# A two-layer graph network on one core: first destinations by way of SBUF, and ten groups of q and v rows instead of five

## The chip, the core and the metric

The kernel runs on one core of one Trainium2 chip. A core has TensorE (PE, with its weight loads listed apart as PEld), VectorE (DVE), ScalarE (ACT), GpSimd (POOL) and SyncE (SP), each with an instruction queue of its own, and 16 DMA engines that all queues share. SBUF and PSUM are its on-chip memories of 128 partitions; tables lie in HBM. The metric is the device time of one execution in microseconds. Other measurements of the text come from one profiled execution.

## What is computed

There are 30,000 nodes with 128 features and 960,000 edges, sorted by destination. Cut to what matters:

```python
# layer 0: two relational convolutions, 32 edge types made of 8 bases
h   = relu(layernorm(x))
W   = einsum('rb,bdf->rdf', coeff, basis)
agg = segment_sum((h @ W[etype32])[src] * norm, dst)     # once, relu, once more
x   = x + agg2
# layer 1: gated convolution, 4 edge types
h   = relu(layernorm(x))
k, q, v = h @ Wk[t] + bk[t], h @ Wq[t] + bq[t], h @ Wv[t] + bv[t]
msg = sigmoid(k[dst] + q[src]) * v[src]                  # of the edges with edge_type_4 == t
agg_t = segment_sum(msg, dst)
x   = x + mean over t of (agg_t + h @ Ws[t] + b[t])
```

Everything is float32. (The masked sum over t lets each edge take only the tables of its own type.)

## The kernel before

Edges are cut into tiles of 128 and groups of three tiles (384 edges). Since edges are sorted, the destinations of a group lie in a window of 32 nodes that begins at the group's first destination; a short preparation checks this, and a slower path, not taken here, stands ready in the other case. Sums are held in one SBUF tile `agg` [128 features x nodes] and a group's result is added at columns `agg[:, base : base + 32]` (`add_windows`, line 356). `base` is known only at run time, so it has to be in a register of the engine that uses it.

Three passes over all edges follow each other (`edge_pass`, lines 727 to 729): c1 and c2 are the two relational convolutions (`rel_body`), g is the gated one (`gate_body`). A pass is a loop of 25 iterations of 100 groups. An iteration is cut into four stages of 25 groups, a stage into five blocks of five groups (index `s`; `S = SB = 5`). The order of the instructions on every engine is written out by hand (`manual_schedule`), and the loop has the staggered kind of iteration sync: engines may be in neighbouring stages, `stage_boundary` marks where one begins and `leave_stage` where each engine waits until it is done with the one before.

At the beginning of a stage `loads(k + 1)` asks on SP's queue for the next stage's tiles of indices and relative destinations (`stage_tile`, one tile of each name per stage, `bufs=NQ=4`). `bases` (line 345) brings the first destinations of a stage's 25 groups from row `i*NQ + k` of `first_st` in HBM to 25 registers of one engine:

- in c1 and c2 on DVE, at the fourth group of a stage's second block (group 8 of 25);
- in g on DVE, at the fifth group of a stage's first block (group 4), and once more on SP in `window` (line 478), which fetches a group's 128 key rows (`kw`) from the k table, five groups ahead.

In c1 and c2 a group is: POOL gathers three times 128 rows of h by index (`hg`, line 114, 5 buffers of a group each); DVE builds for each tile a selection matrix times coefficients (`sb`, line 439, 12 buffers); PE multiplies (`pa`); ACT copies to `ab`; once per block PE multiplies by the bases (`po`, line 407) and two blocks later DVE adds the windows.

In g a group is: POOL gathers three times 128 rows of q and v (`qv[n]`, 1 KB a row, 5 buffers of a group each, line 533); PE selects keys by a one-hot matrix (`keys`, line 499, from `kb` that DVE makes of a broadcast 960 KB load per block, `onehot`, line 486); DVE adds q (line 540); ACT takes the sigmoid (line 541). Two groups later DVE multiplies by v (`msg`, line 508), which is the last use of `qv[n]`, and PE sums (`po`, line 510). So DVE's order in iteration step n is: add of group n, product of group n - 2, then, by position in the block, one-hot, windows, `bases`.

Beside the groups run the steps of the node work of the pass before (`beside`), 120 nodes at a time.

Of the kernel before, what the change touches and what calls it, by code (L numbers as in the profile page):

```python
# [9 lines left out]
F32 = mybir.dt.float32  # L10
# [21 lines left out]
G = 3  # L32
# [37 lines left out]
def kernel(  # L70
# [223 lines left out]
    def sorted_path():  # L294
        with ExitStack() as all_:
# [46 lines left out]
                nc.sync.dma_start(t, array[:, ds(i * (NQ * NTS) + k * NTS, NTS + more)])  # L342
                return t

            def bases(i, k, engine):
                _, vals = nc.values_load_multi_w_load_instructions(
                    first_st[ds(i * NQ + k, 1), :NGS], engines=[engine],
                    min_val=0, max_val=N - 1, skip_runtime_bounds_check_because=IN_RANGE)
                return vals

# [10 lines left out]
            def rel_body(table, weights, cof):  # L361
                def start(npool):
                    bas = npool.tile([P, B, D], F32, name="bas")
                    nc.scalar.dma_start(bas, weights.rearrange("b d f -> d b f"))
                    return lambda *args: body(bas, *args)

                def body(bas, i, io, pool, ps, cp, iw, ic, beside):
                    stage = {}
                    er, oh, pc, ce, ab, po, base = {}, {}, {}, {}, {}, {}, {}

                    def loads(k):
                        stage[k] = [stage_tile(io, "idx", src, I32, i, k),
                                    stage_tile(io, "relc", reld, F32, i, k),
                                    stage_tile(io, "nrm", norm, F32, i, k, 4 * TQ - S * G)]

                    def types(s):
                        er[s] = pool.tile([P, TQ, TP], I32, name="er")
                        nc.sync.dma_start(
                            er[s].rearrange("p c e -> p (c e)"),
                            bass.AP(tensor=et32_row.tensor, offset=(i * NG + s * S) * GE,  # L380
                                    ap=[[TQ * TP, 4], [0, R], [1, TQ * TP]]))

                    def onehot(s):
                        oh[s] = pool.tile([P, TQ, TP], F32, name="oh")
                        nc.vector.tensor_scalar(oh[s], er[s], icol4, None, op0=ALU.is_equal)
                        at = (1 + s % 2) * TQ * 4 * B
                        pc[s] = cp[:TP, at:at + TQ * 4 * B].rearrange("p (c q b) -> p c q b",
                                                                      c=TQ, q=4)
                        for c in range(TQ):
                            nc.tensor.matmul(pc[s][:, c].rearrange("p q b -> p (q b)"),  # L390
                                             lhsT=oh[s][:, c, :],
                                             rhs=cof.rearrange("p q b -> p (q b)"),
                                             start=True, stop=True)

                    def coefficients(s):
                        ce[s] = pool.tile([TP, 4, TQ, B], F32, name="ce")
                        t0 = s % SB * S * G
                        nrm = stage[s // SB][2][:, t0:t0 + 4 * TQ]
                        nc.vector.tensor_mul(
                            ce[s], pc[s].rearrange("p c q b -> p q c b"),  # L400
                            nrm.rearrange("p (q c) -> p q c", q=4).unsqueeze(3).to_broadcast(
                                [TP, 4, TQ, B]))

                    def bases_out(s):
                        po[s] = ps.tile([P, S, W], F32, name="po")
                        for b in range(B):
                            nc.tensor.matmul(po[s].rearrange("p s w -> p (s w)"),  # L407
                                             lhsT=bas[:, b, :],
                                             rhs=ab[s][:, b].rearrange("p s w -> p (s w)"),
                                             start=(b == 0), stop=(b == B - 1))  # L410

                    loads(0)
                    types(0)
                    onehot(0)
                    coefficients(0)
                    types(1)
                    onehot(1)
                    for s in range(NS):
                        k = s // SB
                        if s % SB == 0:  # L420
                            if s:
                                tc.stage_boundary()
                            if k + 1 < NQ:
                                loads(k + 1)
                        if s % SB == 2:
                            leave_stage()
                        idx, relc, _ = stage[k]
                        if s + 2 < NS:
                            types(s + 2)
                        ab[s] = pool.tile([P, B, S, W], F32, name="ab")  # L430
                        for g in range(S):
                            t0 = (s % SB * S + g) * G
                            hg = pool.tile([TP, G, D], F32, name="hg", bufs=5)
                            for j in range(G):
                                gather(hg[:, j, :], table, idx[:, t0 + j:t0 + j + 1])
                            pa = ps.tile([P, B, W], F32, name="pa", bufs=3)
                            for j in range(G):
                                sb = pool.tile([TP, B, W], F32, name="sb", bufs=12)
                                nc.vector.scalar_tensor_tensor(  # L439
                                    sb, iw[:TP].unsqueeze(1).to_broadcast([TP, B, W]),  # L440
                                    relc[:, t0 + j:t0 + j + 1],
                                    ce[s].rearrange("p q c b -> p (q c) b")[
                                        :, g * G + j, :].unsqueeze(2).to_broadcast([TP, B, W]),
                                    op0=ALU.is_equal, op1=ALU.mult)
                                nc.tensor.matmul(pa.rearrange("p b w -> p (b w)"),  # L445
                                                 lhsT=hg[:, j, :],
                                                 rhs=sb.rearrange("p b w -> p (b w)"),
                                                 start=(j == 0), stop=(j == G - 1))
                            nc.scalar.copy(ab[s][:, :, g, :], pa)  # L449
                            if g == 1 and s:  # L450
                                bases_out(s - 1)
                            if g == 2 and s + 1 < NS:
                                coefficients(s + 1)
                            if g == 3 and s + 2 < NS:
                                onehot(s + 2)
                            if g == 3 and s > 1:
                                add_windows(po[s - 2], base[(s - 2) // SB], s - 2)
                            if g == 3 and s % SB == 1:
                                base[k] = bases(i, k, DVE)
                            beside(s * S + g)  # L460
                    bases_out(NS - 1)
                    for s in (NS - 2, NS - 1):
                        add_windows(po[s], base[NQ - 1], s)
                return start

            def gate_body(i, io, pool, ps, cp, iw, ic, beside):
# [1 line left out]
                kb, kw, sel, pk, qv, po, base, kbase = {}, {}, {}, {}, {}, {}, {}, {}  # L468

                def loads(k):  # L470
                    stage[k] = [stage_tile(io, *a, i, k) for a in (
                        ("qi", qidx, I32), ("relc", reld, F32))]

                def types(s):
# [3 lines left out]
                def window(n):  # L478
                    k = n // NGS
                    if n % NGS == 0:  # L480
                        kbase[k] = bases(i, k, SP)
                    kw[n] = pool.tile([P, D], F32, name="kw", bufs=10)
                    nc.sync.dma_start(kw[n], ktab[ds(kbase[k][n % NGS] * T, P), :])

                def onehot(s):
# [2 lines left out]
                                            ALU.is_equal)  # L488
                    sel[s] = pool.tile([TP, S * G, W], F32, name="sel", bufs=3)
                    t0 = s % SB * S * G  # L490
                    relc = stage[s // SB][1][:, t0:t0 + S * G]
                    nc.vector.tensor_tensor(
                        sel[s], iw[:TP].unsqueeze(1).to_broadcast([TP, S * G, W]),
                        relc.unsqueeze(2).to_broadcast([TP, S * G, W]), ALU.is_equal)
# [25 lines left out]
                for n in range(NG):  # L520
# [9 lines left out]
                        types(s + 1)  # L530
                    if n + S < NG:
                        window(n + S)
                    qv[n] = pool.tile([TP, G, 2, D], F32, name="qv", bufs=5)
                    t0 = n % NGS * G
                    for j in range(G):
                        gather(qv[n][:, j].rearrange("p a f -> p (a f)"), qvtab,
                               stage[k][0][:, t0 + j:t0 + j + 1])
                    if n + 1 < NG:
                        keys(n + 1)
                    nc.vector.tensor_add(pk[n], pk[n], qv[n][:, :, 0, :])  # L540
# [5 lines left out]
                    if g == 4 and s:  # L546
                        add_windows(po[s - 1], base[(s - 1) // SB], s - 1)
                    if g == 4 and s % SB == 0:
                        base[k] = bases(i, k, DVE)
                    beside(n)  # L550
                sums(NG - 2)
                sums(NG - 1)
# [409 lines left out]
```

## Time and profile before

| | |
|---|---|
| Time, median of 3 runs | 28,902.54 us (28,895.52 to 28,908.87) |
| The profiled execution's own time | 34,449.25 us |
| Its span, first to last instruction | 34,447.5 us |
| Mean granted clock of TensorE | 0.674 (0.74 in c1, 0.78 in c2, 0.51 in g) |
| Gathers of POOL in c1, c2, g | 192.6 to 11,387.4; 11,431.9 to 22,748.0; 22,865.2 to 34,419.9 us |
| POOL busy in the three stretches | 7149, 7118, 7109 us |
| DMA engines' mean busy share | 0.23, 0.26, 0.47 |
| PE busy in g | 6756 of 11,555 us |

A line of the page's groups names source line, engine, operation, what is written and read, the count, then busy time and the mean of one in ns, then the idle time just before and what ended most of it. In the waits, a row is who waited for whom, the total in us, how often, and the longest. A timeline's line has start, duration, engine, line, operation, and in brackets the idle time before it and its releaser. "issue" means that the profile shows nothing that was waited for, "remote" that the releasing semaphore is known but not the instruction. A busy gather on POOL is the time in which POOL works on it, not the time until the rows have landed.

### The profile page before, as it was taken

To read this page: it belongs to the slowest core of one execution; us is meant where nothing else is said; L and a number is where in the kernel's file an instruction comes from. 1 tells how busy PE (TensorE), PEld (TensorE's weight loads), DVE (VectorE), ACT (ScalarE), POOL (GpSimd) and SP (SyncE) were. 2 spreads that over 40 slices of the span, in tenths; PEclk is the share of its full clock that TensorE was granted. 3 is DMA by queue.
4 is the path that set the end of the run, shared out by engine and by line. 5 is a ranking of instruction groups with operands and counts; after the bars stand their busy time and mean duration, and the time that the engine had idled before them with its cause. 6 is when DMAs were issued, how large, how long until landed. Compare 5 with 4: busy or idle time off the path is not lost. (4 is left out here: it accounts for less than half of the span.)

```text
span 34447.5 us, 320361 instructions
## 1 busy us (share of the span) xinstructions
PE 20497.2 (60%) x87408; PEld 17662.1 (51%) x87408; DVE 12592.8 (37%) x33274; ACT 3659.3 (11%) x9905; POOL 21410.1 (62%) x22514
## 2 busy tenths in 40 slices
PE   4555555555555566666666666665555555555555
PEld 3444544444444445545555454445555555555555
DVE  3333333333333333333333333333333333333333
ACT  1000000000000111111111111111111111111111
POOL 5666666666666566666666666656666666666666
PEclk7777777777777777777777777765555555555555
DMA  3222222222222222222222222234444444444444
GB/s 97 62 62 62 63 61 62 63 63 62 62 62 62 70 73 73 73 74 72 72 73 73 73 73 73 73 107 145 145 144 144 144 144 146 145 144 144 146 143 141
DMA packets 2182999, 3244.35 MB, mean 94 GB/s; under 512 B 551918, under 2 KB 1559594, under 8 KB 2181290
## 3 DMA queue, kind: packets, MB, share of 16 engines
q0 software_dynamic: 840000, 1967.52, 20.6%
q1 hardware_dynamic: 993620, 1001.65, 9.0%
q10 hardware_dynamic: 347670, 254.20, 2.6%
q8 instruction: 852, 13.96, 0.2%
q14 instruction: 857, 7.02, 0.1%
HBM read 2969.29 MB, written 252.28 MB: 94 GB/s over the span
## 5 line engine op out<-in xcount | busy, mean ns | idle before, releaser
L114 POOL DMA_INDIRECT hg<-h,idx x15000 | 14273.0, 952 | 8446.5 <-issue 4105.1
L445 PE MATMUL pa<-sb,hg 128*128 128x256 f32 x30000 | 9304.2, 468 | 5934.2 <-issue 2892.9
L445 PEld LDWEIGHTS pa<-sb,hg 128*128 128x128 f32 x30000 | 6919.2, 240 | 7715.2 <-issue 3346.1
L114 POOL DMA_INDIRECT qv<-qvtab,qi x7500 | 7109.3, 948 | 4562.6 <-issue 2220.3
L439 DVE SCALAR_TENSOR_TENSOR sb<-cp,relc,ce 128x256 f32<-128x256 f32 x15000 | 6134.1, 476 | 6576.0 <-remote 4679.9
L510 PE MATMUL po<-sel,msg 128*128 128x32 f32 x15000 | 3471.0, 388 | 4592.1 <-DVE msg L508 3824.5
L510 PEld LDWEIGHTS po<-sel,msg 128*128 128x128 f32 x15000 | 3420.4, 328 | 4894.5 <-DVE msg L508 3986.6
L499 PE MATMUL pk<-kw,kb 128*128 128x128 f32 x15000 | 3973.5, 438 | 219.5 <-DVE kb L486 178.4
L540 DVE TENSOR_TENSOR pk<-pk,qv 128x384 f32<-128x384 f32 x2500 | 1406.8, 563 | 7074.9 <-remote 4837.9
L449 ACT COPY ab<-pa 128x256 f32<-128x256 f32 x5000 | 1816.6, 373 | 20148.8 <-remote 8809.6
L499 PEld LDWEIGHTS pk<-kw,kb 128*128 128x128 f32 x15000 | 3466.7, 331 | 222.3 <-issue 222.3
L407 PE MATMUL po<-ab,bas 128*128 128x160 f32 x16000 | 2431.3, 306 | 311.2 <-ACT ab L449 262.8
L407 PEld LDWEIGHTS po<-ab,bas 128*128 128x128 f32 x16000 | 2356.8, 196 | 408.4 <-ACT ab L449 291.0
L359 DVE TENSOR_TENSOR agg<-agg,po 128x32 f32 x7500 | 1402.9, 187 | 2742.5 <-remote 709.7
L541 ACT ACTIVATE pk<-pk 128x384 f32<-128x384 f32 x2500 | 1186.7, 475 | 9493.7 <-DVE pk L540 6531.3
L390 PE MATMUL cp<-coeff,oh 128*128 128x32 f32 x8000 | 1313.4, 297 | 1472.0 <-issue 1173.2
L390 PEld LDWEIGHTS cp<-coeff,oh 128*128 128x128 f32 x8000 | 1394.2, 237 | 1530.9 <-issue 1308.1
L637 PE MATMUL bank<-wall,hT 128*120 128x512 f32 x1572 | 1012.0, 765 | 710.2 <-issue 307.3
L508 DVE TENSOR_TENSOR msg<-pk,qv 128x384 f32<-128x384 f32 x2500 | 1368.0, 548 | 19.4 <-remote 19.4
L486 DVE TENSOR_TENSOR kb<-kb,cp 128x1920 f32<-128x1920 f32 x500 | 1072.7, 2145 | 52.0 <-issue 29.6
L637 PEld LDWEIGHTS bank<-wall,hT 128*120 128x120 f32 x1572 | 345.9, 235 | 988.0 <-issue 581.2
L648 DVE TENSOR_TENSOR kt<-bank,ball 120x512 f32<-120x512 f32 x262 | 181.2, 692 | 1484.0 <-remote 509.2
(77 smaller groups left out, 3762.9 us busy)
## 6 DMA issues: line engine op xcount, KB each, us to landing
kb<-kcode SPq DMA_DIRECT2D x500, 960.0 KB
er<-in_et_row SPq DMA_DIRECT2D x1000, 256.0 KB
hg<-h,idx POOLq DMA_INDIRECT x15000
kw<-ktab SPq DMA_DIRECT2D x2500, 64.0 KB
qvtab<-qvt ACTq DMA_DIRECT2D x262, 480.0 KB
qv<-qvtab,qi POOLq DMA_INDIRECT x7500
ktab<-kt ACTq DMA_DIRECT2D x262, 240.0 KB
xt<-in_x SPq DMA_DIRECT2D x262, 60.0 KB
```

Of the source, the lines that this page charges most:

```text
L114: nc.gpsimd.indirect_dma_start(out=to, out_offset=None, in_=table, in_offset=bass.IndirectOffsetOnAxis(ap=idx, axis=0))
L359: nc.vector.tensor_add(to, to, po[:, g, :])
L390: nc.tensor.matmul(pc[s][:, c].rearrange("p q b -> p (q b)"), lhsT=oh[s][:, c, :], rhs=cof.rearrange("p q b -> p (q b)"), start=True, stop ...
L407: nc.tensor.matmul(po[s].rearrange("p s w -> p (s w)"), lhsT=bas[:, b, :], rhs=ab[s][:, b].rearrange("p s w -> p (s w)"), start=(b == 0), ...
L439: nc.vector.scalar_tensor_tensor(sb, iw[:TP].unsqueeze(1).to_broadcast([TP, B, W]), relc[:, t0 + j:t0 + j + 1], ce[s].rearrange("p q c b - ...
L445: nc.tensor.matmul(pa.rearrange("p b w -> p (b w)"), lhsT=hg[:, j, :], rhs=sb.rearrange("p b w -> p (b w)"), start=(j == 0), stop=(j == G ...
L449: nc.scalar.copy(ab[s][:, :, g, :], pa)
L499: nc.tensor.matmul(pk[n][:, j, :], lhsT=kb[n // S][:, n % S, j * TP:(j + 1) * TP], rhs=kw[n], start=True, stop=True)
L508: nc.vector.tensor_mul(msg, pk[n], qv[n][:, :, 1, :])
L510: nc.tensor.matmul(po[s][:, g, :], lhsT=msg[:, j, :], rhs=sel[s][:, g * G + j, :], start=(j == 0), stop=(j == G - 1))
L540: nc.vector.tensor_add(pk[n], pk[n], qv[n][:, :, 0, :])
L637: nc.tensor.matmul(bank(a, VB, T * D), lhsT=hT, rhs=wall[:, a].rearrange("p t f -> p (t f)"), start=True, stop=True)
```

## The change

It has two parts. First, `firsts` is new: with each stage's tiles SP now loads the stage's row of `first_st` (32 int32 values, 128 bytes) into an SBUF tile of one partition, and `bases` fills the registers from that tile instead of from HBM. The row is the last of a stage's loads in c1 and c2 and the first of them in g, which moves the places of the other tiles in `stage[k]` by one. Second, the pool of `qv` tiles in g has ten buffers instead of five.

```diff
-            def bases(i, k, engine):
+            def firsts(io, i, k):
+
+                t = io.tile([1, 32], I32, name="firsts")
+                nc.sync.dma_start(t, first_st[ds(i * NQ + k, 1), :])
+                return t
+
+            def bases(t, engine):
                 _, vals = nc.values_load_multi_w_load_instructions(
-                    first_st[ds(i * NQ + k, 1), :NGS], engines=[engine],
+                    t[:, :NGS], engines=[engine],
...
                         stage[k] = [stage_tile(io, "idx", src, I32, i, k),
                                     stage_tile(io, "relc", reld, F32, i, k),
-                                    stage_tile(io, "nrm", norm, F32, i, k, 4 * TQ - S * G)]
+                                    stage_tile(io, "nrm", norm, F32, i, k, 4 * TQ - S * G),
+                                    firsts(io, i, k)]
...
-                        idx, relc, _ = stage[k]
+                        idx, relc, _, start = stage[k]
...
-                                base[k] = bases(i, k, DVE)
+                                base[k] = bases(start, DVE)
...
-                    stage[k] = [stage_tile(io, *a, i, k) for a in (
+                    stage[k] = [firsts(io, i, k)] + [stage_tile(io, *a, i, k) for a in (
                         ("qi", qidx, I32), ("relc", reld, F32))]
...
-                        kbase[k] = bases(i, k, SP)
+                        kbase[k] = bases(stage[k][0], SP)
...
-                    qv[n] = pool.tile([TP, G, 2, D], F32, name="qv", bufs=5)
+                    qv[n] = pool.tile([TP, G, 2, D], F32, name="qv", bufs=10)
...
-                               stage[k][0][:, t0 + j:t0 + j + 1])
+                               stage[k][1][:, t0 + j:t0 + j + 1])
...
-                        base[k] = bases(i, k, DVE)
+                        base[k] = bases(stage[k][0], DVE)
```

More of the change, by code (lines that the diff above doesn't have):

```diff
@@ L490, in onehot @@
                     t0 = s % SB * S * G
-                    relc = stage[s // SB][1][:, t0:t0 + S * G]
+                    relc = stage[s // SB][2][:, t0:t0 + S * G]
                     nc.vector.tensor_tensor(
```

## The prediction, made before the changed kernel had run

> **What bounds the kernel now.** I read the page's engine table first, then the groups, then the three passes as stretches, then the timeline of POOL, because POOL issues every gather.
>
> ```profile
> PE 20497.2 (60%) x87408; PEld 17662.1 (51%) x87408; DVE 12592.8 (37%) x33274; ACT 3659.3 (11%) x9905; POOL 21410.1 (62%) x22514
> ...
> L114 POOL DMA_INDIRECT hg<-h,idx x15000 | 14273.0, 952 | 8446.5 <-issue 4105.1
> ...
> L114 POOL DMA_INDIRECT qv<-qvtab,qi x7500 | 7109.3, 948 | 4562.6 <-issue 2220.3
> ```
>
> 22,500 gathers carry POOL. Its timeline in the third pass (start, busy time, what ended the idle time) gives their pace:
>
> ```profile
> 27077.59 0.95 POOL L114 DMA_INDIRECT qv<-qvtab,qi  x1 [0.30 <-issue]
> 27078.85 0.94 POOL L114 DMA_INDIRECT qv<-qvtab,qi  x1 [0.30 <-issue]
> 27083.89 0.95 POOL L114 DMA_INDIRECT qv<-qvtab,qi  x1 [4.10 <-DVE msg L508]
> 27085.15 0.95 POOL L114 DMA_INDIRECT qv<-qvtab,qi  x1 [0.30 <-issue]
> ```
>
> Two things are to be seen. Unstalled, gathers start 1.25 us apart (0.95 busy, 0.30 between), so a group of three takes 3.76 us. And now and then POOL stops for some 4 us until DVE has freed a buffer of q and v rows. The waits of POOL in the third pass:
>
> ```profile
> POOL qv L114 <- issue: 2220.3, 6716, 4.5
> ...
> POOL qv L114 <- DVE msg L508: 1761.6, 473, 15.1
> ...
> POOL qv L114 <- DVE pk L540: 349.3, 144, 5.1
> ```
>
> 6716 x 0.30 = 2015 of the first row is the plain step. The DVE rows, less 617 x 0.30 = 185 us, are 1.93 ms of stalls; 473 of them against 500 blocks of five groups is about one a block. By spans: the third pass's gathers run from 22865 to 34420 us, 11,555 us, where 7500 x 1.2525 = 9394 would do, so 2.16 ms are stalls. The first pass (193 to 11,387) has 1.80 ms over its 9394, the second (11,432 to 22,748) 1.92 ms. Together 5.88 ms.
>
> **But this profile is of a slowed execution.** It took 34,449 us, the runs without profile 28,902 at the median: 5.55 ms less. That is nearly the sum of all stalls. Put the other way: 22,500 x 1.2525 = 28,181 us of gathers, plus what lies around them (193 before the first, 45 and 117 between passes, 28 after the last: 383), is 28,564 us. Only 28,902 - 28,564 = 338 us are left for every stall of all three passes in a run without profile. The stalls look like the recording's own. This is DVE around the stall above, then PE:
>
> ```profile
> 27077.68 0.65 DVE L492 TENSOR_TENSOR sel<-cp,relc 128x480 f32<-128x480 f32 x1
> 27082.60 0.57 DVE L540 TENSOR_TENSOR pk<-pk,qv 128x384 f32<-128x384 f32 x1 [4.27 <-remote]
> 27083.08 0.55 DVE L508 TENSOR_TENSOR msg<-pk,qv 128x384 f32<-128x384 f32 x1
> ```
>
> ```profile
> 27077.06 1.63 PE L499 MATMUL pk<-kw,kb 128*128 128x128 f32 x6
> 27083.68 0.64 PE L510 MATMUL po<-sel,msg 128*128 128x32 f32 x2 [4.99 <-DVE msg L508]
> ```
>
> PE's last work ended at 27078.69, DVE's at 27078.33, POOL had gathered ahead, and yet DVE began only at 27082.60, let go by "remote", not by a named engine. 4837.9 us of DVE's idle time before L540 have that label. Whether the 1.25 us of a gather are stretched by the recording too, the profile cannot say; that is the main fork below.
>
> **What the Trainium skill says.** "DMA: Bandwidth & Descriptors", section "Latency and other measured facts", puts the floor of a register load at about 600 ns. "Runtime: NRT & Kernel Launch", section "Instruction fetch mechanics", gives about 200 ns a register from HBM even in bulk. The trace roughly agrees with the first and undercuts the second: DVE's load of 25 values is 3433 ns at the median, 137 ns a value.
>
> ```profile
> L346 DVEq TENSOR_LOAD <-in_first_st_ptr x300: 891/955/3095, 221.4 to 34332.8; - x150
> ...
> L346 DVEq TENSOR_LOAD <-in_first_st x300: 3127/3433/6490, 222.9 to 34335.0; - x150
> ```
>
> "Perfetto Trace Analysis", section "Per-engine timelines", says that the end of a POOL-issued DMA in a profile is the end of descriptor generation, not of the data. So the 0.95 us is POOL's own work, which more buffers don't shorten; no view here contradicts it.
>
> **The change, part by part.**
>
> *Removed:* per stage and engine one load of a pointer (DVE 955, SP 1760 ns), register arithmetic (69 + 48 ns) and a load of 25 values from HBM (DVE 3433, SP 3916 ns). With gaps of about 0.2 that is 4.7 us on DVE, 300 times, and 6.0 us on SP, 100 times: 1.41 ms and 0.60 ms of sequencer time.
>
> *Added:* 300 DMAs of one 128-byte row on SP's queue. The stage tiles beside them take 0.33 us each to issue at the median, with 0.05 + 0.03 for address and move: 0.41 x 300 = 123 us of SP. And 400 register loads from SBUF. The only such loads in the trace are the flag's, one value each:
>
> ```profile
> L249 SPq TENSOR_LOAD <-flag x1: 478/478/478, 55.9 to 55.9; - x1
> ...
> L249 DVEq TENSOR_LOAD <-flag x1: 816/816/816, 183.3 to 183.3; - x1
> ```
>
> For 25 values the low end is that (0.5 to 0.8 us), the middle end the HBM load of as many (3.4), the high end 25 single loads in a row (12 us on SP, 20 on DVE). I take 2.2 us, between the first two, since the pointer's load falls away and a value from HBM costs 137 ns at most. DVE saves about 2.5 us a stage, 0.75 ms in all.
>
> *What hides that.* In the first two passes DVE writes 12 sb tiles ahead, four groups, 15 us of POOL's pace; a stop of 4.7 us at group 8 of 25 is inside it. In the third pass DVE is idle 63% of the time and stops once in 25 groups, while POOL's stalls come once in five; they don't follow the loads. So I cost this part at nothing on the path; if the cover were gone, it would be 0.75 ms the good way. On SP the loads stand before key windows fetched five groups (19 us) ahead: nothing too.
>
> *Waits added.* DVE and SP now wait for the row's landing. It is issued a stage (94 us) ahead, except in stage 0. There, in the rel passes, DVE asks nine groups (34 us) later. In the third pass the row is the first thing on SP's queue; behind it are qi and relc, then kb, which in the iteration before 27030 waited from 26999.8 to 27013.7 for its buffer, and only then the register load. Behind that load the five kw DMAs queue, and PE's keys wait for those. The row has 14 us to land: nothing. The first gather of the pass waits for qi, now 0.4 us later: nothing.
>
> *Ten q/v buffers.* POOL may now start group n when DVE has multiplied group n-10, not n-5. Behind the gathers of group n, DVE adds group n, then multiplies n-2, which frees the buffer. With five, group n+5 waits for the landing of n+2, 3 groups or 11.3 us after that one's start; three gathers, the landing and 1.1 us of DVE use about 6.5 of it, so a delay above some 4.8 us stalls POOL. With ten that is 23.6 us. What can be late: kb's 960 KB once in five groups, onehot (2.15 + 0.65 us), and the turn of the loop, where DVE must end the last window, branch, build onehot and two sets of keys before group 5. All are below 23.6 us, so the DVE stalls go. DVE (36% busy), PE (58%) and the DMA engines (47%, all three over the pass's stretch) have room to catch up. What is late next is nothing but POOL's own step.
>
> In the profiled execution this is worth most of 1.93 ms, to a span of about 32.6 ms. In a run without profile there are 338 us of stalls in three passes. By the profile's shares the third has 2.16 / 5.88 = 37%, 124 us, of which the DVE rows are 1.93 / 2.16 = 89%: **111 us**. Sum: 28,902 - 111 - 0 + 0 = 28,791 us, 0.4% less. Differences under 0.2% (58 us) are about what a measurement of this kernel can't tell from none.
>
> **Rivals.**
>
> *No measurable change.* Without the recording's delays the 4.8 us of slack may already cover the third pass: by hand, the turn of the loop takes 7.4 us from an iteration's first gather (1.6 until the last rows of the old one land, 2.1 for DVE's two sums and products, 1.5 for PE, 1.3 for the windows, 0.9 for the branch) and then 9.9 to 11.4 us from onehot to the freed buffer (two turns read from the timeline), 17.3 to 18.8 in all, and POOL gets there after 18.75. Then the 338 us belong to the first two passes (the turn there is longer: the stalls at group 5 are 5.8 and 9.0 us on average, 24 times each, 355 us), and the gain is 0 to 50 us: 28,870. For it: that sum. Against: it leaves the third pass nothing at all.
>
> *The recording stretches the gathers, the stalls are real.* Then POOL's true step is (28,902 - 383 - 5880) / 22,500 = 1.006 us, the third pass really loses about 1.9 ms, and 28,902 - 1,900 = 27,000 us follows. For it: the rows say plainly that POOL waits for DVE. Against: it needs stalls that are as long without profile as with it, and DVE's idle time with all its inputs there.
>
> *The register load is slow.* If SBUF values come one after another at the flag's price, DVE stops for 25 x 0.816 = 20.4 us. The point from which it decides is the 15 us that the sb tiles cover; 5.4 us over it, in 200 stages of the first two passes, is 1.08 ms: 29,870 us. For it: the single price. Against: the same instruction brings 25 values from HBM in 3.4 us, so a value can't cost 0.8.
>
> **How the numbers follow.** The likeliest, 48%: a gain of 60 to 210 us around 111, so 28,690 to 28,842. No change, 32%: 28,845 to 28,960. Real stalls, 11%: 26,900 to 28,400. Slow loads or another loss, 9%: above 28,960. Faster is 48 + 11 = 59%, same 32%, slower 9%. The first two cases hold 80%; I widen to 28,250 and 29,000 for the ends of the others.
>
> **What would show it.** In the profile after, the row of the third pass's waits for DVE should fall from 473 times to some tens, its 11,555 us to near 9,600, the passes before it should stay within 1%; the HBM loads of L346 should be replaced by shorter ones without a pointer. A fall of the runs' time as large as the span's would show that the stalls were real. Wrong would be: third pass's stalls that stay with another releaser (a gather's own landing, kb), or a first pass that moves.

## The result, and the profile after

| | before | after |
|---|---|---|
| Time, median (range) | 28,901.8 us (28,895.52 to 28,908.87, 4 runs) | 28,699.47 us (28,692.62 to 28,713.88, 4 runs) |
| Ratio | | 0.9931, 95% interval 0.9919 to 0.9944 |
| Span of a profiled execution | 34,447.5 us (shown above); 28,901.0 us (a second one) | 28,694.1 us |
| Device time of that execution | 34,449.25; 28,902.76 us | 28,695.83 us |
| Gathers of c1, c2, g, from first to last (second profile; after) | 9,426; 9,414; 9,673 us | 9,434; 9,416; 9,454 us |

The change saves 202 us, 0.7%. The profile shown before the prediction and the times beside it don't belong together: on the chip of the first experiments every execution of the kernel before takes 28.9 ms, with and without profile, while on three other chips every one takes 34.2 ms. So the first profile is compared below with those chips, and the second profile of the kernel before (first experiment) with after.

The engine table and the two groups of gathers, after:

```profile
PE 21423.9 (75%) x87408; PEld 17175.0 (60%) x87408; DVE 12662.0 (44%) x33274; ACT 3718.3 (13%) x9905; POOL 21329.2 (74%) x22514
...
L114 POOL DMA_INDIRECT hg<-h,idx x15000 | 14212.2, 947 | 4846.7 <-issue 3865.1
...
L114 POOL DMA_INDIRECT qv<-qvtab,qi x7500 | 7089.3, 945 | 2488.5 <-issue 2063.6
```

POOL's busy time is what it was (21,410 us in the first profile, 21,333 in the second). What shrank is the idle time before the qv gathers: 4562.6 us in the first profile, 2700.1 in the second, 2488.5 after, of which 2063.6 is the plain step between two gathers.

POOL's waits, after (total us, how often, longest us):

```profile
POOL qv L114 <- issue: 2063.6, 6690, 1.2
POOL qv L114 <- DMA qv<-qvtab,qi: 176.8, 412, 2.2
...
POOL qv L114 <- DVE msg L515: 33.4, 108, 0.8
```

The row of waits for DVE's product, which held 473 waits and 1761.6 us in the first profile and 250 waits and 268.8 us in the second, is 108 waits of 0.31 us on average, the plain step: hardly anything is lost there any more. POOL's timeline at the place where the kernel before stops longest, group 5 of an iteration (first gather at 23008.05):

```profile
23005.55 0.94 POOL L114 DMA_INDIRECT qv<-qvtab,qi  x1 [0.30 <-issue]
23006.80 0.95 POOL L114 DMA_INDIRECT qv<-qvtab,qi  x1 [0.30 <-issue]
23008.05 0.95 POOL L114 DMA_INDIRECT qv<-qvtab,qi  x1 [0.30 <-DMA qv<-qvtab,qi]
23009.30 0.95 POOL L114 DMA_INDIRECT qv<-qvtab,qi  x1 [0.30 <-issue]
```

It runs through at 1.25 us. The register loads, after (count, then min/median/max in ns):

```profile
L352 DVEq TENSOR_LOAD <-firsts x300: 1834/1846/2586, 217.6 to 28597.0; - x150
...
L352 SPq TENSOR_LOAD <-firsts x100: 1821/1838/2022, 19211.1 to 28551.6; - x100
```

25 values from SBUF take 1.85 us on either engine, and the pointer's load is gone.

A "stall" below is the time by which the step from one gather's start to the next exceeds the median step of the same pass (1.249, 1.249 and 1.251 us in c1, c2 and g); longer steps alone are summed over the pass. In the second profile of before the stalls are 66, 54 and 298 us; after, 75, 57 and 82 us. All of the gain is in the third pass.

### The profile page after: what moved, and what is told of

It reads as the page before. It is cut to its first block, busy times and chain, and to the rows that moved or that the text cites. A ratio compares the mean times of both kernels' runs of the same rounds, so it can differ in the third digit from the quotient of the medians.

```text
span 28694.1 us, 321544 instructions
## 1 busy us (share of the span) xinstructions
PE 21423.9 (75%) x87408; PEld 17175.0 (60%) x87408; DVE 12662.0 (44%) x33274; ACT 3718.3 (13%) x9905; POOL 21329.2 (74%) x22514
## 3 DMA queue, kind: packets, MB, share of 16 engines
q1 hardware_dynamic: 994220, 1001.69, 10.8%
## 5 line engine op out<-in xcount | busy, mean ns | idle before, releaser
L452 PE MATMUL pa<-sb,hg 128*128 128x256 f32 x30000 | 9879.9, 460 | 4210.1 <-DMA hg<-h,idx 2911.0
L452 PEld LDWEIGHTS pa<-sb,hg 128*128 128x128 f32 x30000 | 6016.4, 223 | 7340.5 <-issue 3683.7
L114 POOL DMA_INDIRECT qv<-qvtab,qi x7500 | 7089.3, 945 | 2488.5 <-issue 2063.6
L517 PE MATMUL po<-sel,msg 128*128 128x32 f32 x15000 | 3551.9, 393 | 2400.1 <-DVE msg L515 2394.2
L414 PEld LDWEIGHTS po<-ab,bas 128*128 128x128 f32 x16000 | 2859.8, 230 | 144.7 <-ACT ab L456 50.8
L414 PE MATMUL po<-ab,bas 128*128 128x160 f32 x16000 | 2883.9, 344 | 23.1 <-ACT ab L456 23.1
L397 PEld LDWEIGHTS cp<-coeff,oh 128*128 128x128 f32 x8000 | 1313.8, 235 | 452.5 <-issue 328.0
L397 PE MATMUL cp<-coeff,oh 128*128 128x32 f32 x8000 | 1229.3, 304 | 358.8 <-DVE oh L392 358.8
L644 PE MATMUL bank<-wall,hT 128*120 128x512 f32 x1572 | 911.2, 697 | 9.0 <-issue 4.6
L392 DVE TENSOR_SCALAR oh<-er,icol 128x512 f32<-128x512 int32 x1000 | 490.6, 491 | 88.8 <-issue 62.7
```

Source lines behind the costliest of these rows:

```text
L114: nc.gpsimd.indirect_dma_start(out=to, out_offset=None, in_=table, in_offset=bass.IndirectOffsetOnAxis(ap=idx, axis=0))
L414: nc.tensor.matmul(po[s].rearrange("p s w -> p (s w)"), lhsT=bas[:, b, :], rhs=ab[s][:, b].rearrange("p s w -> p (s w)"), start=(b == 0), ...
L452: nc.tensor.matmul(pa.rearrange("p b w -> p (b w)"), lhsT=hg[:, j, :], rhs=sb.rearrange("p b w -> p (b w)"), start=(j == 0), stop=(j == G ...
L517: nc.tensor.matmul(po[s][:, g, :], lhsT=msg[:, j, :], rhs=sel[s][:, g * G + j, :], start=(j == 0), stop=(j == G - 1))
```

## The experiments

Two theories stood first. A: the gain is that of ten buffers in the third pass. B: it is that of the register loads. The first four kernels ran on one chip, where before takes 28,889.49 us (25 runs).

**The kernel before, again**, without an edit, for a profile on the chip that gives the times.

> The kernel before, unchanged, recorded once more. If the stalls of the first recording were the recording's own (as the prediction has it), they may be absent or smaller this time: a span near 28,900 us, a gather step of 1.25 us, and about 340 us of POOL's stalls over the three passes, some 120 us of them in the third. If the stalls were real and gathers are stretched by the recording, the span is again near 34,400 us, or the step falls towards 1.0 us.

Measured: 28,890.47 us, ratio 1.0 (0.999 to 1.0009), span 28,901.0 us. Its waits of POOL in the third pass:

```profile
POOL qv L114 <- issue: 2013.5, 6451, 1.3
...
POOL qv L114 <- DVE msg L508: 268.8, 250, 6.3
...
POOL qv L114 <- DMA qv<-qvtab,qi: 166.7, 383, 2.2
```

250 waits for DVE, of which 250 x 0.30 = 75 us are the plain step: 194 us of stalls, a tenth of the 1.93 ms of the first profile. Taken by the place in the iteration of 100 groups, 239 of the third pass's 298 us sit in three places: group 5 (3.90 us on average, 25 times: 97 us); groups 33, 58 and 83 (1.15, 1.11 and 1.29 us: 89 us); groups 37 and 62 (0.60 and 1.53 us: 53 us). The rest is spread thinly. Group 5 is the turn of the loop:

```profile
23068.06 0.39 SPq L476 DMA_DIRECT2D kb<-kcode  x1
...
23075.09 0.56 DVE L540 TENSOR_TENSOR pk<-pk,qv 128x384 f32<-128x384 f32 x1 [6.75 <-DMA qv<-qvtab,qi]
...
23082.73 2.15 DVE L486 TENSOR_TENSOR kb<-kb,cp 128x1920 f32<-128x1920 f32 x1 [1.23 <-issue]
...
23091.75 0.54 DVE L508 TENSOR_TENSOR msg<-pk,qv 128x384 f32<-128x384 f32 x1
...
23092.56 0.95 POOL L114 DMA_INDIRECT qv<-qvtab,qi  x1 [4.30 <-DVE msg L508]
```

The iteration's first gather starts at 23069.48. DVE adds the old iteration's last group only 5.6 us later, since its rows land late, while the kb load issued just before is under way. The first one-hot follows 13.2 us after that gather, and the product that frees the buffer ends at 23092.3, so POOL, which would be there after 18.75 us, starts group 5 after 23.1.

The stalls at groups 33, 58 and 83 are the register loads'. DVE's queue and then the timeline, at group 33 of the same iteration:

```profile
L346 DVEq TENSOR_LOAD <-in_first_st_ptr x1: 921/921/921, 23193.7 to 23193.7; - x1
...
L346 DVEq TENSOR_LOAD <-in_first_st x1: 3378/3378/3378, 23194.9 to 23194.9; - x1
```

```profile
23198.47 0.56 DVE L540 TENSOR_TENSOR pk<-pk,qv 128x384 f32<-128x384 f32 x1 [4.57 <-DMA qv<-qvtab,qi]
23198.94 0.55 DVE L508 TENSOR_TENSOR msg<-pk,qv 128x384 f32<-128x384 f32 x1
...
23199.76 0.95 POOL L114 DMA_INDIRECT qv<-qvtab,qi  x1 [1.57 <-DVE msg L508]
```

From 23193.7 to 23198.3 DVE's queue is in the two loads. The view puts the idle time before L540 down to the landing of the rows; the queue shows that the loads ended last. At all 75 such places of the pass the add that follows starts about 0.2 us after the end of the second load. The next product ends at 23199.5 and POOL starts 1.27 us late.

**Rows alone, in all three passes**, five buffers.

```diff
-                    qv[n] = pool.tile([TP, G, 2, D], F32, name="qv", bufs=10)
+                    qv[n] = pool.tile([TP, G, 2, D], F32, name="qv", bufs=5)
```

> Register loads from SBUF in all three passes, five buffers of q and v as before. Theory A (the prediction: the gain lies in the buffers of the third pass): within 58 us of before, about 28,900 us. Theory B (the register loads hold DVE up where POOL has no cover): most of the 202 us of gain, about 28,700 to 28,760 us. Half and half: 28,800 us.

Measured (the edit is against after): 28,771.55 us, 0.9961 (0.9948 to 0.9975), 118 us less than before. Stalls of the third pass 158 us. Group 5 stays at 3.88 us; groups 33, 58 and 83 lose theirs, 37 and 62 all but 0.1 us.

```profile
POOL qv L114 <- DVE msg L515: 162.1, 214, 4.8
```

**Ten buffers alone**, registers from HBM.

```diff
-                    qv[n] = pool.tile([TP, G, 2, D], F32, name="qv", bufs=5)
+                    qv[n] = pool.tile([TP, G, 2, D], F32, name="qv", bufs=10)
```

> Ten buffers of q and v, register loads from HBM as before. Theory A: the whole gain, about 28,700 to 28,760 us. Theory B: about 28,900 us. If each part gives half, this and the kernel with the rows alone both stand near 28,800 us and the gains add up to 202 us.

Measured (against before): 28,738.13 us, 0.9949 (0.9935 to 0.9962), 151 us less. Stalls of the third pass 140 us: group 5 and groups 33, 58 and 83 are gone, groups 37 and 62 have 1.40 and 1.67 us, 77 us together, and what POOL waits for there is the landing of gathers before:

```profile
POOL qv L114 <- DMA qv<-qvtab,qi: 220.0, 454, 2.3
...
POOL qv L114 <- DVE msg L508: 44.8, 146, 0.5
```

So both theories hold in part. 118 + 151 - 202 = 67 us are gained by either part; with intervals of some 36 to 39 us on each of the three this fits the stalls that both remove, those of groups 33, 58 and 83 (89 us). Only the buffers remove group 5, only the rows groups 37 and 62.

**Rows in the first two passes alone.** The third pass is that of before.

```diff
-                                base[k] = bases(i, k, DVE)
+                                base[k] = bases(start, DVE)
...
                     def loads(k):
...
+                                    firsts(io, i, k)]
```

> Register loads from SBUF in the first two passes alone; the third pass loads from HBM and has five buffers. Theory A: as before, 28,900 us. Theory B with the loss in the first two passes (200 of DVE's 300 loads): as the kernel with rows in all passes, about 28,700 to 28,760 us; with the loss in the third pass's DVE and SP loads: 28,900 us.

Measured: 28,894.48 us, 1.0002 (0.9994 to 1.0011); stalls 70 and 57 us against 66 and 54. There the shorter loads are worth nothing that can be measured.

The next four were to tell DVE's load from SP's and to ask whether still more buffers help. They ran on a chip where before takes 34,188.23 us (47 runs).

**DVE's row alone in the third pass, five buffers; SP's row alone; DVE's row with ten buffers.** The engine that is not named loads from HBM as before.

```diff
-                        base[k] = bases(i, k, DVE)
+                        base[k] = bases(stage[k][0], DVE)
```

```diff
-                        kbase[k] = bases(i, k, SP)
+                        kbase[k] = bases(stage[k][0], SP)
```

> Third pass only: DVE fills its registers from the SBUF row, SP still from HBM, five buffers. Theory D (DVE's HBM load holds the products back, so the buffers come free late): the stalls at groups 33, 58 and 83 go, 85 to 90 us, a time of 28,800 to 28,815; those at 37 and 62, some 50 us, stay. Theory P (SP's HBM load makes the queue behind it late): no gain, 28,880 to 28,900. If DVE's load is the cause of both kinds, 28,765 to 28,780 as with both rows.

> Third pass only: SP fills its registers from the SBUF row, DVE still from HBM, five buffers. Theory D: the stalls at 33, 58 and 83 stay; at most the 25 to 50 us at groups 37 and 62 go, where SP's load puts the kb load off: 28,840 to 28,890. Theory P: all of the rows' gain is here, 28,765 to 28,785.

> As the first, with ten buffers. With ten, DVE's hold no longer reaches POOL, and what the rows still bring (39 us, from 28,738 to 28,699) must come from SP's queue if theory P holds for the rest: then this is 28,730 to 28,745. If it is DVE's load that puts off the kb load through the one-hot's freeing of kb, this is 28,695 to 28,710.

**Fifteen buffers in the changed kernel.**

```diff
-                    qv[n] = pool.tile([TP, G, 2, D], F32, name="qv", bufs=10)
+                    qv[n] = pool.tile([TP, G, 2, D], F32, name="qv", bufs=15)
```

> The changed kernel with fifteen q and v buffers. If what is left (about 82 us of stalls in the third pass) no longer comes from the buffers but from POOL's own step and from gathers that wait for the landing of earlier ones: within 0.1% of ten, 28,680 to 28,715. If the buffers still hold, as much again as a part of the 82 us: 28,620 to 28,660.

Measured: 34,176.01 us, 0.9994 (0.9985 to 1.0002); 34,128.33 us, 0.9982 (0.9975 to 0.9989); 34,184.68 us, 0.9998 (0.9989 to 1.0006); 34,230.10 us, 1.0011 (1.0003 to 1.002). Two of them, the first and the last, ran once more, on a further chip where before takes 34,188.15 us:

> The same kernel as the first of the set before (third pass: DVE's registers from the row, SP's from HBM, five buffers), which ran where every kernel took 34.2 ms. If the chip runs the kernel before at 28.9 ms, theory D (DVE's load holds the products back): ratio 0.9965 to 0.9972, 28,790 to 28,810, with the stalls at groups 33, 58 and 83 gone and those at 37 and 62 left; theory P (SP's load): ratio 0.999 to 1. If the chip runs at 34.2 ms: 0.999 to 1, as before.

> The changed kernel with fifteen q and v buffers, again. Where the kernel before takes 28.9 ms: within 0.1% of ten, ratio 0.992 to 0.994, if what is left is POOL's own step; 0.990 to 0.991 if buffers still hold. Where it takes 34.2 ms: 1.000 to 1.002, as before.

Measured: 34,163.10 us, 0.9995 (0.9986 to 1.0003); 34,236.97 us, 1.0014 (1.0007 to 1.0021). Every expectation for 28.9 ms is left without an answer; those of the two repeated runs for 34.2 ms were met. None of these runs tells DVE's load from SP's where it matters, and why SP's row alone gains 60 us there is not explained. What they do tell is that stalls of the first profile's size are no matter of buffers: the third pass has 2,140 us of them with five (DVE's row), 2,162 with ten and 2,185 with fifteen.

**The changed kernel itself on such a chip**, and the changed kernel with a fifth of the edge codes' load: per block 192 KB instead of 960, repeated for the five groups by the one-hot, so four fifths of the codes are left out and the keys are others.

```diff
-                    nc.sync.dma_start(kb[s], edge_row(kcode, i, s, P))
+                    kc[s] = pool.tile([P, 1, GE + GAP], F32, name="kc")[:, :, :GE]
+                    nc.sync.dma_start(kc[s], bass.AP(
+                        tensor=kcode.tensor, offset=(i * NG + s * S) * GE,
+                        ap=[[0, P], [GE, 1], [1, GE]]))
...
-                    nc.vector.tensor_tensor(kb[s], kb[s],
+                    nc.vector.tensor_tensor(kb[s], kc[s].to_broadcast([P, S, GE]),
```

> The changed kernel itself, unchanged, beside the kernel before. Where the kernel before takes 34.2 ms: the kernels around it (rows of DVE alone with ten buffers 0.9998, all with fifteen 1.001) put it at 0.999 to 1.001, no gain from either part, because POOL waits for DVE once a block with any number of buffers; if the earlier reading of the profile before were right (ten buffers absorb those stalls), 0.94 to 0.95. Where the kernel before takes 28.9 ms: 0.993 again.

> The changed kernel with the edge codes of one group loaded per block (192 KB) in place of five (960 KB) and repeated by the one-hot, which leaves out four fifths of that load and so computes other keys. Theory K (the 960 KB burst holds up SP's and DVE's instructions once a block): where the kernel before takes 34.2 ms, the third pass falls from about 11,540 to 9,450 to 10,200 us, so a time 1.3 to 2.1 ms below the changed kernel; where it takes 28.9 ms, the 82 us of stalls left in the third pass shrink, 20 to 80 us below the changed kernel. Theory S (the stalls come from somewhere else, the key windows or the instructions' own supply): the same as the changed kernel within 0.2%.

Measured, beside 34,199.08 us of before (29 runs): 34,163.79 us, 0.999 (0.9981 to 0.9998), and 34,114.20 us, 0.9977 (0.997 to 0.9984). Third pass 11,553 and 11,464 us. So the change is worth 0.1% there, not 0.7% and not the 1.8 ms that the prediction gave for the slower execution; and the 960 KB burst is not the cause of these stalls (theory K falls: of 2.1 ms of stalls the pass lost 89 us). What a block looks like there with ten buffers (the changed kernel, third pass):

```profile
27443.23 1.63 PE L506 MATMUL pk<-kw,kb 128*128 128x128 f32 x6
...
27443.63 9.82 SPq L490 DMA_DIRECT2D kw<-ktab  x5
...
27443.96 1.07 DVE L365 TENSOR_TENSOR agg<-agg,po 128x32 f32 x5
...
27455.68 0.57 DVE L547 TENSOR_TENSOR pk<-pk,qv 128x384 f32<-128x384 f32 x1 [10.65 <-remote]
27456.15 0.55 DVE L515 TENSOR_TENSOR msg<-pk,qv 128x384 f32<-128x384 f32 x1
...
27456.97 0.94 POOL L114 DMA_INDIRECT qv<-qvtab,qi  x1 [3.51 <-DVE msg L515]
```

And the same issue of five key windows in the kernel after, on the chip of the first runs:

```profile
23014.03 2.47 SPq L490 DMA_DIRECT2D kw<-ktab  x5
```

Five DMA issues of SP take 9.8 us instead of 2.5, and DVE stands for 10.65 us. Such a block is some 12 us of DVE's and PE's work and some 10 us of standing, 22.5 us (DVE's resumptions at 27433.17 and 27455.68), and POOL needs 15 x 1.25 = 18.75. The difference, 3.75 us, is POOL's stall, once a block, whether five, ten or fifteen buffers lie between (at group 83 it is 3.75, 3.70 and 3.61 us on average).

What DVE stands for can be read further than "remote". The keys that this add needs are made by the line of PE above, which ended at 27444.86 (ends of matmuls are modelled in the profile); DVE's queue had passed its waits for the rows' landings by 27444.97. The one wait left is for a semaphore of PE. So it is in general in that run (total us, how often, longest):

```profile
DVE pk L547 <- remote: 5011.1, 590, 15.1
```

By the trace's records of semaphores all 590 of these waits end with one of PE's, at the median 10.8 us after the matmuls of these keys, and 9.1 us after the queue's last other wait. On the first chip no add of any of the five kernels profiled there waits for "remote"; on the slower chips 515 to 662 do in each execution. What comes late on the slower chips is thus PE's signal, not PE's work; why it does is not shown.

## Why the prediction was right, and where it was wrong

- **The bound (POOL's 22,500 steps of 1.2525 us, 28,564 us with what lies around).** Right. The steps are 1.249, 1.249 and 1.251 us: 7,500 x 3.749 = 28,118, and 391 us lie around them (193, 45, 124, 29): 28,509 us. The kernel before had 28,901 - 28,509 = 392 us above that, 338 predicted.
- **The stalls of the first profile are not in the runs that are timed.** Right, and the rival of 27,000 us falls with it: where before took 28.9 ms a second profile has 418 us of stalls in three passes instead of 5.9 ms. But "the recording's own" is wrong: the second profile's execution took 28,902.76 us, as the runs without profile do, and on three chips all runs of before without profile take 34.2 ms. On which chip the first profile was taken is not on record; its passes and its waits for "remote" look like those of the slower chips, though at 34,449 us it is 0.6% above their longest run of before (34,248). The comparison of one profile with times taken elsewhere could not tell a slowed recording from a slower chip.
- **"In the profiled execution this is worth most of 1.93 ms, to a span of about 32.6 ms."** Wrong. The changed kernel's span on a slower chip is 34,208.2 us. The step that failed is the sum of slack, 3 groups against 8: it treats each stall as a delay that is made up for afterwards. On these chips DVE loses some 10 us in nearly every block, waiting for PE's late signal, and is slower than POOL on the average, 22.5 us to 18.75, so five, ten and fifteen buffers all fill up. "Have room to catch up" was read from busy shares, but DVE and PE hand each group to one another, and in the block shown that chain fills the 12 us that are not standing.
- **111 us for the buffers.** That deeper buffers take in DVE's delays is right, the term was too small: 151 us alone. The 124 us of the third pass came from its share in the first profile, 37%. In the second it is 298 of 418 us, 71%. The share had been taken from stalls of another origin, so that 111 comes within a factor of two of the measured 202 is luck in good part. Of the delays that it named, the turn of the loop was there (97 us); the next largest that the buffers took in, DVE's register loads (89 us), it had put at nothing.
- **The turn of the loop by hand (the rival of no change, 17.3 to 18.8 us).** Wrong in one term: DVE's one-hot begins 13.0 us after the iteration's first gather (mean of 24 turns), not 7.4, because the last group's add comes 5.4 us after that gather, where 1.6 us was taken for the landing of its rows; they land while the kb load is under way. The second term, 9.9 to 11.4 us, is nearly right (9.6 us on average). POOL reaches group 5 after 22.85 us on average, and with ten buffers after 19.2.
- **Register loads, 2.2 us for 25 values.** Close: 1.85 us. The slow-load rival is excluded. The Trainium skill's floor of about 600 ns ("DMA: Bandwidth & Descriptors", section "Latency and other measured facts") is no floor here: the 25 values lie above it, but SP's single flag load, 478 ns, lies below, and the measurement decides. The 200 ns a register of the Trainium skill's "Runtime: NRT & Kernel Launch", section "Instruction fetch mechanics", are again not reached from HBM (3402 / 25 = 136 ns in the second profile), and from SBUF it is 74.
- **"Nothing on the path" for the loads.** Right for c1 and c2 (1.0002 with the rows there alone). Wrong for the third pass, where the rows are worth 118 us with five buffers and 202 - 151 = 51 us with ten (a difference not much larger than the intervals of the two runs; the stalls of the traces, 140 and 82 us, give 58). "They don't follow the loads" was said of a profile whose own stalls, once in five groups, hid those of groups 33, 58 and 83; by the prediction's own 4.8 us of slack, a stop of 4.6 us on DVE with a group to wait for lies on the edge. That it is DVE's load is shown by the trace for groups 33, 58 and 83. For groups 37 and 62 it is argued only: with HBM loads the kb loads of the blocks that begin with groups 40 and 65 are issued 0.4 to 1.7 us later on average, and POOL waits there for late landings. Whether DVE's load or SP's puts it off was asked and is open.
- **Row DMAs and waits added, nothing.** Nothing against it: the first gather of the third pass comes 124 us after the last of the second, where it was 117 us in the first profile of before and 122 in the second, and c1 and c2 are within 8 us.
- **What would show it.** The row of waits for DVE fell (from 250 in the second profile to 108), the passes before stayed within 0.1% of the second profile, the loads are shorter and without a pointer. The third pass is 9,454 us, below the 9,600 named.

The sum of before, 28,902 - 111 - 0 + 0, reads with measured terms 28,902 - 151 - 51 = 28,700; since 51 is what is left of the 202, this sum had to close. The saving of 202 us lies in the likeliest case (60 to 210 us), at its edge.

## What to carry to other kernels

Buffers take in delays that are made up for later; before pricing deeper buffers, compare how long a whole block takes the consumer with how long it takes the producer, for a stall that comes back in every block at the same size (3.6 to 3.75 us here, with five, ten and fifteen buffers) is a rate and stays. A few microseconds of register loads on an engine that has to free a buffer are to be held against the slack at that place, not against its mean idle share. And when a profile and the times differ by 19%, take a second profile where the times come from before reading any stall: shares of stalls don't carry over.

## What was not expected of the hardware

Chips differ, by 18% for this kernel: 28.9 ms on one, 34.2 ms on three others, at 0.723 and 0.674 mean granted clock, with gathers at the same 1.249 to 1.254 us. The clock is not what slows the third pass: it is granted at 0.51 in that pass on both kinds of chip, and a matmul of the keys takes 438 and 437 ns. What differs in the traces, beside PE's late signals, is how fast SP's queue gets through plain instructions. The register moves of SP before the key windows (min/median/max in ns), after on the first chip, and then the same kernel on one of the others:

```profile
L490 SPq MOVE kw<-ktab x2500: 29/29/37, 19213.2 to 28629.5; - x193
```

```profile
L490 SPq MOVE kw<-ktab x2500: 2/29/1407, 22618.8 to 34160.3; - x193
```

On the first chip SP's records start between 0.66 and 0.74 us apart 32 to 82 times in an execution, on the others 3,641 to 5,475 times, in stretches of several records, and 3,766 times in the first profile. In the block shown above DVE stands, waiting for PE's signal, while SP's issues crawl; whether one causes the other or both have a third cause is not shown. Neither the registers' source, nor the buffers, nor the bytes of the kb load take it away. Its cause is open, the supply of the instructions themselves among the possible ones that no run here tests.
